# Layer-1 selective scans of a two-layer vision state-space model: decay in PSUM, B in single PSUM banks, the product with C on GpSimd

## The chip, the cores and the metric

The kernel runs on one core of a Trainium2 chip. The metric is the device time of one execution in microseconds (us). Before the change the median of three timed runs is 46,708.61 us (46,704.51 to 46,712.61).

In the profile the engines are PE (TensorE: matrix products), PEld (its loads of weights), DVE (VectorE), ACT (ScalarE), POOL (GpSimd) and SP (SyncE, which issues transfers). Each engine works through its own queue in program order and waits on semaphores for the others.

## The reference, cut to what matters

The input is an image batch, 4 x 128 x 128 pixels with 192 channels. Two residual layers follow each other; each is normalised in groups, projected, convolved, scanned and projected back. The change concerns the scan of layer 1. There every one of 192 channels has 16 states and is scanned in four directions over L = 16,384 tokens (by rows, by rows backwards, by columns, by columns backwards):

```python
def step(state, inp):
    d, b, c, uu = inp
    dA = jnp.exp(d[..., None] * A_neg[:, None, :, :])
    state = dA * state + (d * uu)[..., None] * b[:, :, None, :]
    y = jnp.einsum('kbcn,kbn->kbc', state, c)
    return (state, y)
```

For a channel and a state n: the decay is exp(A * delta), the increment delta * u * B, the output the sum over the 16 states of state times C. B and C depend on token, state, direction and batch, not on the channel. The outputs of the four directions are added. Everything is fp32.

## The kernel before

Layer 0 comes first, then layer 1 in four stages: `in_conv` and `projections` (which write u, delta, B and C of all directions to DRAM), `scans`, and `layer1_out`. Channels lie on the partitions. Layer 1 takes the four batches in two pairs: 2 x 192 channels are three blocks of 128.

`scans` loops over 2 pairs, 3 blocks (i), 4 directions (k), and 16 chunks of T = 1024 tokens: 384 chunks. For each chunk it loads delta (`d`), `u` and 128 rows of B and C (`bt`), and GpSimd forms `du` = d * u (L579). Then it goes through the 16 states n. One state is:

- ScalarE: `dA` = exp(d * A_n) (L593), 128 x 1024, into SBUF (pool `r_3`, three buffers).
- TensorE: row n of B broadcast to the 128 partitions, by a product of `bt` with a column of the identity, stretched over 128 columns (or with `pick` for block 1): `g`, two PSUM banks of 512 columns, from the helper `mm` (L95); pool `r_ps`, two buffers.
- VectorE: `h` = du * g (L605).
- VectorE: the scan `h` = dA * h(previous token) + h, along the tokens (L607), starting from the last value of the chunk before, `st`.
- GpSimd: the last column of `h` copied to `st` for the next chunk (L613).
- VectorE: `hc` = h * C (L617). C comes as `ct`, broadcast by a transfer over the partitions, two states at a time, three buffers (L586).
- TensorE: `hc` times the identity, added up over the 16 states in `Y`, two PSUM banks (L619); pool `r_ps`, two buffers.

After the 16 states VectorE adds `Y` to `ysum` in SBUF (L624, L629 or L636, by direction; the two column directions use a strided pattern at L636).

The text names by B(n), scan(n), hc(n) and Y(n) these products of state n. A product of fp32 with 512 columns is two passes of TensorE, so a state is eight passes: four for B, four for Y.

The order of the instructions on each engine is fixed when the program is built: a scheduler places them by their dependences and by which buffers are free, so the number of buffers of a pool decides how far an engine's queue runs ahead in program order. In this kernel's built order TensorE's queue reads B(n+3), Y(n), B(n+4), Y(n+1) and so on: B is three states ahead. `du` of the next chunk is placed on GpSimd among the copies of the chunk in work, and `ysum` of a chunk on VectorE after the first scan of the next chunk.

[...]

Of the kernel before, what the change touches and what calls it, by code (L numbers as in the profile page):

```python
# [17 lines left out]
L = H * W  # L18
R = 8                # image rows in a chunk
T = R * W            # tokens in a chunk  # L20
NCH = L // T
HC = C // 2          # layer 0 keeps the 192 channels as two halves of 96
NB = 3               # layer 0: 384 inner channels, three blocks of 128
PAD = 5              # reach of the widest dilated convolution
HW_ = W + 2 * PAD
NS = 16              # layer 1: states per channel
DR = 12              # both layers: rank of the step-size projection

# Layer 1 takes the batches in pairs: 2 x 192 channels are three full blocks of 128.
# Block 0: channels 0..127 of the first; block 2: of the second;  # L30
# block 1: channels 128..191 of the first, then of the second.
PAIRS = B // 2
# Weights W[192, 192] for such blocks are six [128, 128] tiles (pair_pack); which tile takes
# which input block to each output block:
AA, MA, MC, AM, CM, MM = range(6)
PAIR_TERMS = (((AA, 0), (MA, 1)), ((AM, 0), (MM, 1), (CM, 2)), ((MC, 1), (AA, 2)))

# Columns of the packed per-channel vectors.
V0_CW, V0_CB, V0_DTB, V0_AL, V0_DS, V0_K, V0_G, V0_B, V0_N = 0, 9, 10, 11, 12, 13, 40, 41, 42
V1_CW, V1_CB, V1_G, V1_B, V1_DTB, V1_DS, V1_AL, V1_N = 0, 9, 10, 11, 12, 16, 20, 84  # L40

# The dilated convolutions as (column of the weights, dy, dx); the three centres are one tap.
TAPS = [
# [9 lines left out]
def segments(first, n, dy):  # L53
    """Rows first..first+n-1 moved by dy and clamped to the image, as runs within one chunk:
    (offset among the n, chunk, row in it, rows, whether it is one row repeated)."""
    runs = []
    for i in range(n):
        src = min(max(first + i + dy, 0), H - 1)
        ch, row = divmod(src, R)
        if runs:  # L60
            o, c, r0, cnt, rep = runs[-1]
            if c == ch and row == r0 and (rep or cnt == 1):
                runs[-1] = (o, c, r0, cnt + 1, True)
                continue
            if c == ch and not rep and row == r0 + cnt:
                runs[-1] = (o, c, r0, cnt + 1, False)
                continue
        runs.append((i, ch, row, 1, False))
    return runs
# [16 lines left out]
class Maker:  # L86
# [3 lines left out]
    def mm(self, out, terms):  # L90
        """out [M, 2, 512] = the sum of lhsT.T @ rhs over terms; rhs has 1024 columns."""
        nc = self.nc
        for h in range(2):
            for i, (lhsT, rhs) in enumerate(terms):
                nc.tensor.matmul(  # L95
                    out[:, h], lhsT, rhs[:, h * 512 : (h + 1) * 512],
                    start=(i == 0), stop=(i == len(terms) - 1),
                )

    def softplus(self, pool, x, bias, one):  # L100
        """log(1 + exp(x + bias)) of a PSUM tile, as max(., 0) + log1p(exp(-|.|));
        log1p(u) is ln(w) + (u - (w - 1)) with w the rounded 1 + u."""
        nc = self.nc
# [14 lines left out]
    def gn_finish(self, pool, psum, stats, p96, eps, out):  # L118
        """bn_stats of every channel [96, 2, n, 6] -> out [96, 2, 2]: mean and
        1/sqrt(var + eps) of the channel's group of six."""  # L120
        nc = self.nc
# [15 lines left out]

# [1 line left out]

# [32 lines left out]

# [1 line left out]

    def layer0(self, xT, x1T, gn_in, gn_out, w, ident, p96, eps, one):
        nc, tc = self.nc, self.tc
        ctx = ExitStack()
        with ctx:
# [23 lines left out]

            # -exp(A_logs), in A_logs' place
            al = vec[:, :, V0_AL : V0_AL + 1]
            nc.scalar.activation(al, al, AF.Exp)
            nc.vector.tensor_scalar_mul(al, al, -1.0)
            # the dilated kernels times their alphas, the centres summed
            for d in range(3):
# [16 lines left out]

            def first_half(b, j):
                """Chunk j up to its scan: xn, xs, xd (projections) and hp (the states, with the
                image's edge columns repeated)."""
                r0 = R * j
# [86 lines left out]
            def second_half(b, j, stats):  # L316
                """Chunk j from its dilated convolutions to the layer's output; reads the states
                of the chunks beside it."""
                r0 = R * j
# [96 lines left out]

# [1 line left out]

    @staticmethod
    def block_parts(p, i):  # L420
        """Block i of pair p: (its partitions, batch, channels)."""
        if i == 1:
            return [(slice(0, 64), 2 * p, slice(128, C)), (slice(64, 128), 2 * p + 1, slice(128, C))]
        return [(slice(0, 128), 2 * p + i // 2, slice(0, 128))]
# [11 lines left out]
    def in_conv(self, x1T, gn, xc, win, vec):  # L436
        """xc[o][p][i]: the convolved input of block i, by rows (o = 0) and by columns (o = 1)."""
        nc, tc = self.nc, self.tc
# [71 lines left out]
    def projections(self, xc, delta, bc, xpw, dtw, dtb2, one):  # L510
        """delta[p][i][k]: the step sizes; bc[p][o]: 128 rows of B and C, those of direction
        2 o + kk and batch e of the pair from row 64 kk + 32 e on."""
        nc, tc = self.nc, self.tc
# [31 lines left out]
    def scans(self, xc, delta, bc, y, ident, alog, dsum):  # L545
        """y[p][i]: the four directions' outputs of block i, summed, by rows."""
        nc, tc = self.nc, self.tc
        with tc.tile_pool(name="r_1", bufs=1) as p1, tc.tile_pool(
            name="r_2", bufs=2
        ) as p2, tc.tile_pool(name="r_3", bufs=3) as p3, tc.tile_pool(  # L550
            name="r_ps", bufs=2, space=PSUM
        ) as ps:
            # Block 1 takes B of the first batch to its first 64 partitions, of the second to the rest.
            pick = p1.tile([128, 2, NS, 128], F32, name="pick")
            for kk in range(2):
                for e in range(2):
# [4 lines left out]
                    )  # L561
            NC_ = 2  # states whose C one load brings
            for p in range(PAIRS):
                for i in range(3):
                    ysum = p1.tile([128, L], F32, tag="ysum", name="ysum")
                    for k in range(4):
# [3 lines left out]
                        for at, j in enumerate(order):  # L570
# [8 lines left out]
                            nc.gpsimd.tensor_tensor(du, d, u, ALU.mult)  # L579
                            Y = ps.tile([128, 2, 512], F32, tag="Y", name="Y")  # L580
                            for n in range(NS):
                                if n % NC_ == 0:
                                    ct = p3.tile([128, NC_, T], F32, tag="ct", name="ct")
                                    for part, b, _ in self.block_parts(p, i):
# [6 lines left out]
                                        )  # L591
                                dA = p3.tile([128, T], F32, tag="dA", name="dA")
                                nc.scalar.activation(  # L593
# [5 lines left out]
                                else:  # L599
                                    r = 64 * kk + 16 * i + n  # L600
                                    lhsT = ident[:, r : r + 1].to_broadcast([128, 128])
                                g = ps.tile([128, 2, 512], F32, tag="g", name="g_B")
                                self.mm(g, [(lhsT, bt)])
                                h = p3.tile([128, T], F32, tag="h", name="h")
                                nc.vector.tensor_tensor(h, du, flat(g), ALU.mult)  # L605
                                way = slice(None) if kk == 0 else slice(None, None, -1)
# [4 lines left out]
                                if at < NCH - 1:  # L611
                                    last = T - 1 if kk == 0 else 0
                                    nc.gpsimd.tensor_copy(  # L613
                                        st[:, n : n + 1], h[:, last : last + 1]
                                    )
                                hc = p3.tile([128, T], F32, tag="hc", name="hc")
                                nc.vector.tensor_tensor(hc, h, ct[:, n % NC_], ALU.mult)  # L617
                                for s in range(2):
# [107 lines left out]
def kernel(ctx: ExitStack, tc: tile.TileContext, w: dict, out: bass.AP):  # L726
# [24 lines left out]

    # layer 1
    xc = [
# [20 lines left out]
    nc.sync.dma_start(vec, w["vec1"].rearrange("(k p) v -> p k v", p=128))  # L774
    # -exp(A_logs), in A_logs' place; twice the step sizes' bias; the directions' D summed
    alog = vec[:, :, V1_AL : V1_AL + 4 * NS]
# [19 lines left out]

# [1 line left out]
def pair_pack(w):  # L798
    """[192, 192] -> [128, 6, 128], the tiles AA, MA, MC, AM, CM, MM."""
    t = np.zeros((128, 6, 128), np.float32)  # L800
    t[:, AA] = w[:128, :128]
    t[:64, MA] = w[128:, :128]
    t[64:, MC] = w[128:, :128]
    t[:, AM, :64] = w[:128, 128:]
    t[:, CM, 64:] = w[:128, 128:]
    t[:64, MM, :64] = w[128:, 128:]
    t[64:, MM, 64:] = w[128:, 128:]
    return t


def block_rows(v):
    """Per-channel rows [192, n] -> [256, n]: those of blocks 0 and 2, then those of block 1."""
    return np.concatenate([v[:128], v[128:], v[128:]])
# [80 lines left out]
```

## Time and profile before

| | |
|---|---|
| median of the timed runs | 46,708.61 us |
| span of the profiled execution, first to last instruction | 46,686.2 us |
| what lies around the span, against that median | 22.4 us |
| layer 0 and the first stages of layer 1, up to the first L605 | 15,702 us |
| scans of layer 1 | 29,159 us |
| `layer1_out` | 1,825 us |
| VectorE, busy in the span | 40,417.4 us (87%) |
| TensorE | 36,537.3 us (78%) |
| ScalarE | 14,711.1 us (32%) |
| GpSimd | 4,422.5 us (9%) |
| mean granted TensorE clock | 0.935 |

No time of the profiled execution beside its span is shown, so its own time is taken as the span and those 22.4 us. The slices of the span show the stages:

```profile
PE   6878778777555788788877887788778877787789
DVE  6777777777944799999999999999999999999952
ACT  3323232332399522222222222222222222222235
POOL 0000000000033200010000000000001000000000
PEclk8888888888778899999999999999999999999999
```

Each digit is the busy share, in tenths, of a fortieth of the span (1,167 us). Layer 0 fills slices 1 to 11; the scans begin in slice 14 and fill the digits 9 of DVE; the last two slices are `layer1_out`. PEclk is the clock that was granted to TensorE, in tenths of full speed.

In a group's row the numbers behind the first bar are the busy time in us and the mean of one instruction in ns; behind the second bar stands the idle time of that engine just before these instructions, and what ended most of it. In a row of the timeline the first two numbers are start and duration in us.

### The profile page before, as it was taken

The numbers are of one execution on the slowest core, as the hardware profiler recorded it, in microseconds if no ns is written. First come the engines' busy times: TensorE is split into PE (matmuls) and PEld (weight loads), VectorE is DVE, ScalarE is ACT, GpSimd is POOL, SyncE is SP. The second block draws the span as 40 slices with busy tenths as digits, with TensorE's granted clock in tenths as the row PEclk, the third lists the DMA queues.
The fourth block names the chain that finished last, engine by engine and source line by source line (L and its number), as shares of the span: only waits on it lengthen the run. The fifth ranks groups of instructions, "written<-read, shape, count | busy, mean of one in ns | idle before, by whom it ended". The sixth has DMA issues, their size and how long they took to land. (4 is left out here: it accounts for less than half of the span.)

```text
span 46686.2 us, 265243 instructions
## 1 busy us (share of the span) xinstructions
PE 36537.3 (78%) x86440; PEld 15672.6 (34%) x86440; DVE 40417.4 (87%) x29807; ACT 14711.1 (32%) x13430; POOL 4422.5 (9%) x8170
## 2 busy tenths in 40 slices
PE   6878778777555788788877887788778877787789
PEld 3334334333222233333333333333333333333345
DVE  6777777777944799999999999999999999999952
ACT  3323232332399522222222222222222222222235
POOL 0000000000033200010000000000001000000000
PEclk8888888888778899999999999999999999999999
DMA  3000000000533333345555333333335555433332
GB/s 99 15 16 16 13 16 16 13 16 26 188 133 121 122 134 132 130 138 134 132 131 136 134 132 130 136 133 132 132 130 139 134 130 131 138 133 132 130 109 80
DMA packets 1411883, 4893.13 MB, mean 105 GB/s; under 512 B 122496, under 2 KB 254464, under 8 KB 1410496
## 3 DMA queue, kind: packets, MB, share of 16 engines
q1 hardware_dynamic: 1398208, 4842.60, 33.9%
q0 software_dynamic: 12288, 33.57, 0.3%
q8 instruction: 683, 11.19, 0.1%
q14 instruction: 704, 5.77, 0.0%
HBM read 4338.82 MB, written 536.88 MB: 104 GB/s over the span
## 5 line engine op out<-in xcount | busy, mean ns | idle before, releaser
L607 DVE TENSOR_TENSOR_SCAN h<-dA,st,h 128x1024 f32<-128x1024 f32 x5760 | 14190.3, 2464 | 0.2
L593 ACT ACTIVATE dA<-d,vec 128x1024 f32<-128x1024 f32 x6144 | 7053.0, 1148 | 22089.0 <-DVE h L607 22088.9
L619 PE MATMUL Y<-hc,ident 128*128 128x512 f32 x24576 | 11762.4, 602 | 76.6 <-DVE hc L617 73.8
L95 PE MATMUL g_B<-bt,ident 128*128 128x512 f32 x16384 | 8432.8, 639 | 3884.7 <-DVE h L605 3867.7
L617 DVE TENSOR_TENSOR hc<-h,ct 128x1024 f32<-128x1024 f32 x6144 | 7517.6, 1224 | 0.5
L605 DVE TENSOR_TENSOR h<-du,g_B 128x1024 f32<-128x1024 f32 x6144 | 7329.4, 1193 | 17.2 <-PE g_B L95 17.2
L619 PEld LDWEIGHTS Y<-hc,ident 128*128 128x128 f32 x24576 | 4800.1, 196 | 6277.1 <-issue 6118.7
L95 PEld LDWEIGHTS g_B<-bt,ident 128*128 128x128 f32 x16384 | 2872.2, 194 | 9244.7 <-DVE h L605 6275.6
L95 PE MATMUL g_B<-bt,pick 128*128 128x512 f32 x8192 | 4187.3, 635 | 1886.3 <-DVE h L605 1881.7
L328 PE MATMUL hf<-hp,diag 128*128 128x512 f32 (+3 forms) x14496 | 4569.1, 473 | 261.3 <-ACT hp L307 209.8
L613 POOL COPY st<-h 128x1 f32<-128x1 f32 x5760 | 1180.0, 205 | 24745.4 <-DVE h L607 24743.8
L328 PEld LDWEIGHTS hf<-hp,diag 128*128 128x128 f32 x14496 | 2452.4, 196 | 2205.8 <-issue 1350.3
L95 PEld LDWEIGHTS g_B<-bt,pick 128*128 128x128 f32 x8192 | 1434.4, 193 | 4542.6 <-DVE h L605 3053.5
L344 DVE SCALAR_TENSOR_TENSOR y<-hp,vec,y 128x1024 f32<-128x1024 f32 (+6 forms) x3264 | 2799.2, 900 | 60.5 <-ACT hp L307 54.3
L114 DVE TENSOR_TENSOR sp_l<-sp_l,sp_rl 128x1024 f32<-128x1024 f32 x576 | 967.2, 1679 | 1178.1 <-ACT sp_l L110 1178.1
L278 DVE SCALAR_TENSOR_TENSOR xs<-xi,vec,xs 128x1024 f32<-128x1024 f32 x1536 | 1898.5, 1276 | 2.3 <-DVE y L344 0.2
L95 PE MATMUL g_dt<-pj,dtw 128*128 128x512 f32 x1536 | 970.1, 774 | 1112.7 <-ACT pj L531 742.8
L113 POOL TENSOR_TENSOR sp_r<-sp_u,sp_r 128x1024 f32<-128x1024 f32 x576 | 1523.4, 2645 | 3146.3 <-DVE sp_r L112 3144.9
L95 PE MATMUL g_xd<-xs,xpw 128*128 128x512 f32 x768 | 609.0, 937 | 1183.9 <-ACT xs L282 967.9
L579 POOL TENSOR_TENSOR du<-d,u 128x1024 f32<-128x1024 f32 x384 | 1259.6, 3280 | 1900.8 <-DVE h L605 1778.5
L348 DVE TENSOR_TENSOR y<-y,hf 128x1024 f32<-128x1024 f32 x192 | 231.9, 1208 | 1168.7 <-PE hf L328 1168.7
L363 ACT ACTIVATE sq<-y 128x1024 f32<-128x1024 f32 x192 | 203.0, 1057 | 3050.3 <-DVE y L361 2968.4
(157 smaller groups left out, 27538.7 us busy)
## 6 DMA issues: line engine op xcount, KB each, us to landing
ct<-bc SPq DMA_DIRECT2D x2048, 1024.0 KB, 5.1
ct<-bc SPq DMA_DIRECT2D x2048, 512.0 KB, 6.4
u<-xc SPq DMA_DIRECT2D x576, 512.0 KB, 3.7
delta<-sp_l SPq DMA_DIRECT2D x384, 512.0 KB, 2.6
d<-delta SPq DMA_DIRECT2D x384, 512.0 KB, 3.5
bt<-bc SPq DMA_DIRECT2D x384, 512.0 KB, 3.9
x<-x1T SPq DMA_DIRECT2D x112, 640.0 KB, 5.9
xa<-xT SPq DMA_DIRECT2D x56, 960.0 KB, 5.8
```

The costliest lines, as they stand in the source:

```text
L95: nc.tensor.matmul(out[:, h], lhsT, rhs[:, h * 512 : (h + 1) * 512], start=(i == 0), stop=(i == len(terms) - 1),)
L113: nc.gpsimd.tensor_tensor(r, u, r, ALU.subtract)
L278: nc.vector.scalar_tensor_tensor(a3, xi[:, t // 3 : t // 3 + R, t % 3 : t % 3 + W], v(k, V0_CW + t), a3, ALU.mult, ALU.add,)
L328: nc.tensor.matmul(hf[:, h, o * W : (o + n) * W], diag[:, k, i], rows_of(hp[ch, k], row, n, rep, PAD + dx, W), start=(i == 0), stop=(i == ...
L344: nc.vector.scalar_tensor_tensor(y3[:, o : o + n], src, v(k, V0_K + col), y3[:, o : o + n], ALU.mult, ALU.add,)
L579: nc.gpsimd.tensor_tensor(du, d, u, ALU.mult)
L593: nc.scalar.activation(dA, d, AF.Exp, scale=alog[:, i % 2, k * NS + n : k * NS + n + 1],)
L605: nc.vector.tensor_tensor(h, du, flat(g), ALU.mult)
L607: nc.vector.tensor_tensor_scan(h[:, way], dA[:, way], h[:, way], 0.0 if at == 0 else st[:, n : n + 1], ALU.mult, ALU.add,)
L613: nc.gpsimd.tensor_copy(st[:, n : n + 1], h[:, last : last + 1])
L617: nc.vector.tensor_tensor(hc, h, ct[:, n % NC_], ALU.mult)
L619: nc.tensor.matmul(Y[:, s], ident, hc[:, s * 512 : (s + 1) * 512], start=(n == 0), stop=(n == NS - 1),)
```

## The change

In `scans`, four things, and no other function that computes:

- `dA` is a tile of the PSUM pool `r_ps` (two banks, two buffers) and no longer of SBUF. ScalarE writes it there, the scan reads it there.
- The broadcast of B is made in single banks: for each half of 512 columns a tile `g` [128, 512], one product (L606), and a VectorE multiplication of that half (L607). `g` has two buffers, so two banks in place of four.
- `Y` moves to a pool of its own, `r_ps1`, with one buffer of two banks. [...]
- `hc` = h * C is made on GpSimd (L619 of the changed file) and no longer on VectorE; the copy of the last column into `st` goes from GpSimd to ScalarE (L615).

The scan is at L609 of the changed file, Y's products at L621, `ysum` at L626, L631 and L638. The rest of the diff takes out comments, which moves lines and no instruction.

```diff
         with tc.tile_pool(name="r_1", bufs=1) as p1, tc.tile_pool(
             name="r_2", bufs=2
         ) as p2, tc.tile_pool(name="r_3", bufs=3) as p3, tc.tile_pool(
-            name="r_ps", bufs=2, space=PSUM
-        ) as ps:
+            name="r_ps1", bufs=1, space=PSUM
+        ) as ps1, tc.tile_pool(name="r_ps", bufs=2, space=PSUM) as ps:
...
-                            Y = ps.tile([128, 2, 512], F32, tag="Y", name="Y")
+                            Y = ps1.tile([128, 2, 512], F32, tag="Y", name="Y")
...
-                                dA = p3.tile([128, T], F32, tag="dA", name="dA")
+                                dA = ps.tile([128, T], F32, tag="dA", name="dA")
...
-                                g = ps.tile([128, 2, 512], F32, tag="g", name="g_B")
-                                self.mm(g, [(lhsT, bt)])
                                 h = p3.tile([128, T], F32, tag="h", name="h")
-                                nc.vector.tensor_tensor(h, du, flat(g), ALU.mult)
+                                for s in range(2):
+                                    half = slice(s * 512, (s + 1) * 512)
+                                    g = ps.tile([128, 512], F32, tag="g", name="g_B")
+                                    nc.tensor.matmul(g, lhsT, bt[:, half], start=True, stop=True)
+                                    nc.vector.tensor_tensor(h[:, half], du[:, half], g, ALU.mult)
...
-                                    nc.gpsimd.tensor_copy(
+                                    nc.scalar.copy(
                                         st[:, n : n + 1], h[:, last : last + 1]
                                     )
                                 hc = p3.tile([128, T], F32, tag="hc", name="hc")
-                                nc.vector.tensor_tensor(hc, h, ct[:, n % NC_], ALU.mult)
+                                nc.gpsimd.tensor_tensor(hc, h, ct[:, n % NC_], ALU.mult)
```

## The prediction

> **What bounds the kernel now.** I read the page's groups and slices first, then a table by stretches of time, then the timeline at single steps, because a share over the whole span says nothing of one stage.
>
> The layer-1 scans run from the first to the last multiplication at L605:
>
> ```profile
> core 0: us, PE busy (x) PEld busy (x) DVE busy (x) ACT busy (x) POOL busy (x), PEclk, DMA share, GB/s
> 15702.33:44861.00 29158.67, 23316.69 (x49144) 9104.35 (x49144) 29113.42 (x18821) 7049.80 (x6141) 2432.56 (x6142) 0.98 0.44 133
> ```
>
> VectorE is busy for 29,113 of 29,159 us: it alone sets this stage. There are 2 pairs x 3 blocks x 4 directions x 16 chunks = 384 chunks, so a chunk costs 29,158.67 / 384 = 75.9 us. The groups that make it:
>
> ```profile
> L607 DVE TENSOR_TENSOR_SCAN h<-dA,st,h 128x1024 f32<-128x1024 f32 x5760 | 14190.3, 2464 | 0.2
> ...
> L617 DVE TENSOR_TENSOR hc<-h,ct 128x1024 f32<-128x1024 f32 x6144 | 7517.6, 1224 | 0.5
> L605 DVE TENSOR_TENSOR h<-du,g_B 128x1024 f32<-128x1024 f32 x6144 | 7329.4, 1193 | 17.2 <-PE g_B L95 17.2
> ...
> L579 POOL TENSOR_TENSOR du<-d,u 128x1024 f32<-128x1024 f32 x384 | 1259.6, 3280 | 1900.8 <-DVE h L605 1778.5
> ```
>
> In the timeline equal instructions recur every 4.51 us (L605 at 30002.04 and 30006.55): that is a state. 16 x 4.51 = 72.2; the rest of the 75.9 is `ysum` (1.2 us, or 2.4 at L636) and one blocked scan per chunk:
>
> ```profile
> 30042.61 1.21 DVE L605 TENSOR_TENSOR h<-du,g_B 128x1024 f32<-128x1024 f32 x1
> ...
> 30043.73 1.23 DVE L617 TENSOR_TENSOR hc<-h,ct 128x1024 f32<-128x1024 f32 x1
> 30043.90 3.26 POOL L579 TENSOR_TENSOR du<-d,u 128x1024 f32<-128x1024 f32 x1 [0.88 <-DVE h L605]
> 30044.86 4.45 DVE L607 TENSOR_TENSOR_SCAN h<-dA,st,h 128x1024 f32<-128x1024 f32 x1
> ```
>
> GpSimd's product waits for VectorE's L617 (3.26 us, its shortest is 2.35), then holds up the scan (4.45 for 2.35). Both have two SBUF inputs. With one input in PSUM there is no such block:
>
> ```profile
> 8043.79 2.36 POOL L113 TENSOR_TENSOR sp_r<-sp_u,sp_r 128x1024 f32<-128x1024 f32 x1 [4.39 <-DVE sp_r L112]
> ...
> 8044.99 1.22 DVE L297 TENSOR_TENSOR sp_l<-sp_l,g_B 128x1024 f32<-128x1024 f32 x1 [1.34 <-ACT dA L294]
> ```
>
> **The change, part by part.** (a) L617 leaves VectorE: 1.13 us of its queue per state. (b) dA in PSUM leaves the scan, like the multiplication, one SBUF input, so the pair above says GpSimd runs at 2.35 us beside it and the 2.1 us block per chunk goes. (c) The multiplication in two halves: L344 takes 1.275 us for 1024 elements and 0.742 for 512, so 512 are 0.53 us. From first half to scan are 1.11 - 0.53 = 0.58 and, the second half being awaited at once, 0.80 (worked out below), instead of 1.11: +0.27 per state. (d) The `st` copy goes to ScalarE, behind the next dA and ahead of the one after it: no cost, since ScalarE is 7,050 us busy of 29,159 and dA(n+2) starts some 5 us before its scan; only a lag beyond that would show. VectorE alone would then need 1.38 + 2.26 = 3.64 us per state, TensorE eight passes of 0.43 = 3.44, GpSimd 2.35. No engine is full at 4.5 us. SP's loads of `ct` keep their order and wait on GpSimd instead of VectorE; with three buffers they are issued some 20 us ahead of need, against 5.1 to 6.4 us to landing.
>
> What decides is (e), TensorE's order. In the built order of the changed kernel nearly every state reads: B(n+1) first half, B(n+1) second half, Y(n), B(n+2) first half, and so on. B was three states ahead of Y; with two single banks it is one ahead, B(n+2) stands behind Y(n), and Y(n) now waits for GpSimd's hc(n); behind B(n+2) wait VectorE's halves. So scan n leads to scan n+2 over five engines' hand-overs:
>
> ```profile
> 40047.42 0.30 PEld L619 LDWEIGHTS Y<-hc,ident 128*128 128x128 f32 x2 [2.37 <-DVE hc L617]
> ...
> 40050.96 0.19 PEld L95 LDWEIGHTS g_B<-bt,ident 128*128 128x128 f32 x1 [0.24 <-issue]
> 40051.22 1.22 DVE L605 TENSOR_TENSOR h<-du,g_B 128x1024 f32<-128x1024 f32 x1 [3.86 <-PE g_B L95]
> ...
> 40052.55 2.29 DVE L607 TENSOR_TENSOR_SCAN h<-dA,h 128x1024 f32<-128x1024 f32 x1
> ```
>
> This shows Y's four passes and B's four from the first load to their end, 40050.96: 3.54 us. The link is: scan start to GpSimd start 2.48 (29999.78 to L613 at 30002.26); product 2.35; GpSimd end to the next engine 0.05 (L113 ends 4025.35, ScalarE starts 4025.39); 3.54; to VectorE 0.20 (passes end 3035.55, L348 starts 3035.75); second half to the dependent scan 1.33 - 0.53 = 0.80. Sum 9.42 us for two states. Even states have one wait more in front of hc (the load of `ct`), 0.07 (a scan's end to L613 is 0.13 with an extra wait, 0.06 without): 9.49. So 4.75 us per state, not 3.6: as long as before. Bounds: 0.15 either way for the hand-overs not seen together.
>
> Chunk: 8 x 9.49 = 75.9. `ysum` stands after the next chunk's first scan and delays the odd states: with S0 the end of the chunk's first scan, the second ends at S0 + 4.78 (slots: `ysum` 1.15, 0.58, 0.80, scan 2.34, less 0.08 of overlap), in two directions of four, with the longer `ysum`, at S0 + 5.97. The next `du` is queued on GpSimd between hc(1) and hc(2); then it ends at 5.97 + 0.13 + 2 x 2.35 = S0 + 10.8, where hc(2) could start at S0 + 9.7: +1.1, on the mean +0.55. The single Y costs nothing: `ysum` is done before Y's first passes. Chunk 76.45, so +0.5 x 384 = +0.2 ms, and the whole stage would stay level. One price is missing in this.
>
> (f) TensorE's clock. Before, its idle gaps are 0.81 us; after the blocked scan they are longer:
>
> ```profile
> 30287.13 1.88 PE L619 MATMUL Y<-hc,ident 128*128 128x512 f32 x4
> 30291.50 3.57 PE L95 MATMUL g_B<-bt,ident 128*128 128x512 f32 x4 [2.49 <-DVE h L605]
> ```
>
> After 2.49 us idle four passes took 3.57 instead of 1.98. Laying the trace's clock changes over the gaps between 16.0 and 44.5 ms: the clock goes to half for 3.41 us in 389 places; never where TensorE was idle for under 1.9 us of the 3.41 before, always above 2.25; I take 2.1. It costs nothing now, since VectorE is behind. In the changed kernel these passes are on the path. Evenly spaced, the gaps would be about 1.2 us and harmless. But they will not be even: the chunk's second scan ends 4.78 us after its first, one half of B(3) stands before Y(1), which shortens the odd link by 0.86, and from state 3 on odd scans end 8.56 + 4.78 - 9.49 = 3.85 us after even ones, then 0.07 less per pair down to 3.64, where VectorE's order stops it. The next even scan is then 5.64 to 5.85 away, and TensorE idles in one piece for that less 3.47 (its passes end 6.07 after the odd scan's end, the next Y begins 2.60 after the even one's): 2.2 to 2.4 us. A free 3.41 us stretch holds 2.1 us of such a gap with chance (3.41 - g + 2(g - 2.1)) / 3.41 = 0.41 to 0.47; each time half of 3.41, less up to 0.15, is lost on the path: 1.6 us. 0.7 x 7 pairs = 5.0 us per chunk (the first pair is spaced more evenly). Bounds: 0 (gaps below 2.1) and 0.6 x 1.7 x 8 = 8. I take 5.0, since the spacing follows from the order.
>
> [...]
>
> Sum: chunk 76.45 + 5.0 = 81.45; (81.45 - 75.93) x 384 = +2.1 ms. The profiled execution spans 46,686.2 us, 22.4 below the median of the timed runs; 46,708.6 + 2,120 = 48,830, rounded to 48,800. Its own range: chance of a slow clock 0.3 to 0.6 per pair, links 0.15 either way: 47.8 to 49.8 ms.
>
> **Rivals.**
> 1. Level: the links as summed, states evenly spaced, clock never halved. 46.9 ms, 46.4 to 47.4 with the 0.15. For it: gaps of 2.2 stand close to 2.1. Against: the spacing above.
> 2. Faster: TensorE's queue does not hold B back, and VectorE's 3.6 us per state decide: 16 x 3.6 + 1.7 = 59.3 per chunk, 40.3 ms. It needs a link under 7.2 us, or B issued before Y. Against: the order is fixed in the program, and 9.42 is measured in pieces. Short of it, any link below 9.3 without slow clock is faster too.
> 3. GpSimd is blocked after all by scans (3.26 us instead of 2.35): links of 10.4, gaps of 3.3, slow clock in three pairs of four: about 93 per chunk, 53 ms. Against: 8043.79.
>
> **How the numbers follow.** Forecast 0.55, level 0.22, faster 0.11, blocked 0.07, between level and forecast 0.05. 0.2% (93 us) is about what these runs tell from no change. Level gives slower 0.13, same 0.05, faster 0.04; so slower 0.55 + 0.13 + 0.07 + 0.05 = 0.80, same 0.05, faster 0.15. The range reaches from the low end of level to the high end of the forecast, 46.4 to 49.8 ms; outside stay rivals 2 and 3.
>
> **What would show it.** Right: hc on GpSimd at 2.35 us; VectorE well below 90% busy in the stage, waiting at the halves for TensorE's B; TensorE's loads for Y waiting for GpSimd's hc; scans no longer at 4.4; the clock of the stage down from 0.98 to about 0.9; two states every 10 us. Wrong: VectorE still full, or the mean hc near 3.3, or clock 0.98 with two states in 9.4.

## The result and the profile after

The changed kernel takes 47,953.92 us in the median of four runs (47,950.95 to 47,957.09), the kernel before 46,706.56 (46,699.25 to 46,712.61): 1.0267 times as long, 95% interval 1.0252 to 1.0282. The forecast was 48,800, within 46,400 to 49,800. The profiled execution spans 47,955.3 us, 1,269 more than before. All but some 20 us of it lies in the layer-1 scans, here from the table of busy times by stretches, with the columns that the same table had above:

```profile
15702.00:46110.00 30408.00, 23694.09 (x49149) 9282.89 (x49150) 23170.87 (x18824) 7408.02 (x11912) 15332.92 (x6528) 0.96 0.42 127
```

VectorE was busy for 29,113 of 29,159 us; now it is for 23,171 of 30,408. It has less to do and the stage is longer: no engine is full any more, so the time is in what they wait for. The groups of the page name it:

```profile
L619 POOL TENSOR_TENSOR hc<-h,ct 128x1024 f32<-128x1024 f32 x6144 | 14450.9, 2352 | 15070.0 <-DVE h L609 11084.1
...
L609 DVE TENSOR_TENSOR_SCAN h<-dA,st,h 128x1024 f32<-128x1024 f32 x5760 | 13534.0, 2350 | 611.1 <-DVE h L607 14.7
L607 DVE TENSOR_TENSOR h<-du,g_B 128x512 f32<-128x512 f32 x12288 | 8253.7, 683 | 6566.4 <-PE g_B L606 6019.1
L621 PEld LDWEIGHTS Y<-hc,ident 128*128 128x128 f32 x24576 | 4474.3, 200 | 14649.6 <-POOL hc L619 11072.6
```

Neither side is blocked: the product with C takes 2,352 ns on GpSimd, the scan 2,350 (its mean was 2,464, with one blocked scan per chunk). VectorE waits 6,566 us ahead of the halves, 6,019 of it for B from TensorE; TensorE's loads for Y wait for GpSimd's hc; hc waits for the scan. That is a ring.

The loss is not spread evenly. The same table for pair 0, block 0, one row per direction (rows, rows backwards, columns, columns backwards; the column after the five engines is the granted TensorE clock):

```profile
15713.24:17022.22 1308.98, 1018.95 (x2045) 404.40 (x2044) 951.59 (x788) 308.27 (x496) 638.37 (x272) 0.93 0.35 122
17022.22:18328.83 1306.61, 1017.99 (x2049) 403.78 (x2048) 948.36 (x784) 308.35 (x496) 636.69 (x272) 0.93 0.35 122
18328.83:19549.13 1220.30, 950.71 (x2048) 367.20 (x2046) 981.32 (x784) 308.35 (x496) 638.87 (x273) 1.00 0.38 131
19549.13:20776.95 1227.82, 957.33 (x2049) 370.52 (x2050) 981.76 (x785) 308.32 (x496) 639.66 (x272) 0.99 0.38 129
```

Sixteen chunks take 1,309 and 1,307 us in the row directions at a clock of 0.93, and 1,220 and 1,228 in the column directions at 1.00 and 0.99. Taken over the whole stage from the starts of the scans, a chunk is 81.71 us in the row directions (75.40 before) and 76.60 in the column directions (76.43 before). 192 x 6.31 + 192 x 0.17 = 1,244 us: the row directions carry nearly all of the loss.

What a row direction looks like, in the timeline (start, duration; in brackets the engine's idle time and what ended it):

```profile
16107.44 2.35 DVE L609 TENSOR_TENSOR_SCAN h<-dA,st,h 128x1024 f32<-128x1024 f32 x1
16108.80 1.99 PE L621 MATMUL Y<-hc,ident 128*128 128x512 f32 x4 [2.38 <-POOL hc L619]
...
16111.75 1.48 DVE L607 TENSOR_TENSOR h<-du,g_B 128x512 f32<-128x512 f32 x2 [1.95 <-PE g_B L606]
...
16113.33 2.35 DVE L609 TENSOR_TENSOR_SCAN h<-dA,st,h 128x1024 f32<-128x1024 f32 x1
...
16116.96 2.35 DVE L609 TENSOR_TENSOR_SCAN h<-dA,st,h 128x1024 f32<-128x1024 f32 x1
16118.31 3.60 PE L621 MATMUL Y<-hc,ident 128*128 128x512 f32 x4 [2.25 <-POOL hc L619]
...
16122.96 1.48 DVE L607 TENSOR_TENSOR h<-du,g_B 128x512 f32<-128x512 f32 x2 [3.65 <-PE g_B L606]
16123.54 1.88 PE L621 MATMUL Y<-hc,ident 128*128 128x512 f32 x4
16124.53 2.35 DVE L609 TENSOR_TENSOR_SCAN h<-dA,st,h 128x1024 f32<-128x1024 f32 x1
```

The scans come in bunches of two: 16113.33 and 16116.96 are 3.63 us apart, then a longer pause. In that pause TensorE idles in one piece, 2.38 and 2.25 us. The first gap is followed by passes at full speed (1.99 us), the second by passes at half speed (3.60), and VectorE waits 3.65 us for B instead of 1.95. Two states take 16116.96 - 16107.44 = 9.52 us in the first case, and from 16113.33 to 16124.53 it is 11.20.

In a column direction the same instructions are spaced evenly, TensorE's gaps are about 1 us, and the clock stays up:

```profile
30005.30 1.99 PE L621 MATMUL Y<-hc,ident 128*128 128x512 f32 x4 [0.84 <-POOL hc L619]
...
30010.22 1.98 PE L621 MATMUL Y<-hc,ident 128*128 128x512 f32 x4 [1.22 <-POOL hc L619]
```

Laid over the starts of the scans, the trace's clock changes give the price. A slow window is a stretch of 3.41 us in which the trace has the clock at half; a pair meets one if it begins between the pair's first scan and the next pair's. Of 1,152 pairs of states in row chunks (states 2 to 14), 658 meet no slow window and take 9.52 us in the median; 494 meet one and take 11.20. Of 1,152 pairs in column chunks 26 meet one. A whole row chunk has 3.3 windows, a column chunk 0.2; the 178 column chunks without any take 76.3 us.

### The profile page after: what moved, and what is told of

It reads as the page before. It is cut to its first block, busy times and chain, and to the rows that moved or that the text cites. A ratio compares the mean times of both kernels' runs of the same rounds, so it can differ in the third digit from the quotient of the medians.

```text
span 47955.3 us, 272544 instructions
## 1 busy us (share of the span) xinstructions
PE 36887.1 (77%) x86440; PEld 15856.4 (33%) x86440; DVE 34469.5 (72%) x29807; ACT 15057.7 (31%) x19190; POOL 17314.8 (36%) x8554
## 4 chain that ended last, share of the span: by engine, by line
PE 27%; DVE 16%; POOL 14%; issue 9%; ACT 6%; DMA 1%; POOLq 0%; SPq 0%; DVEq 0%; ACTq 0%
PE Y L621 15%; POOL hc L619 14%; DVE h L609 11%; PE g_B L606 10%; DVE h L607 4%; ACT L108 1%; ACT L110 1%; ACT sp_u L108 1%; ACT sp_u L105 1%; ACT sp_l L110 1%; PE g_dt L95 0%; DMA x<-x1T 0%; PE g_o L702 0%; ACT dA L593 0%; PE g_o L705 0%
## 5 line engine op out<-in xcount | busy, mean ns | idle before, releaser
L619 POOL TENSOR_TENSOR hc<-h,ct 128x1024 f32<-128x1024 f32 x6144 | 14450.9, 2352 | 15070.0 <-DVE h L609 11084.1
L621 PE MATMUL Y<-hc,ident 128*128 128x512 f32 x24576 | 13138.0, 661 | 6635.6 <-POOL hc L619 6620.2
L609 DVE TENSOR_TENSOR_SCAN h<-dA,st,h 128x1024 f32<-128x1024 f32 x5760 | 13534.0, 2350 | 611.1 <-DVE h L607 14.7
L607 DVE TENSOR_TENSOR h<-du,g_B 128x512 f32<-128x512 f32 x12288 | 8253.7, 683 | 6566.4 <-PE g_B L606 6019.1
L621 PEld LDWEIGHTS Y<-hc,ident 128*128 128x128 f32 x24576 | 4474.3, 200 | 14649.6 <-POOL hc L619 11072.6
L606 PE MATMUL g_B<-bt,ident 128*128 128x512 f32 x16384 | 7845.5, 599 | 61.6 <-DVE h L607 51.8
L615 ACT COPY st<-h 128x1 f32<-128x1 f32 x5760 | 1103.2, 192 | 21543.2 <-DVE h L609 21543.2
L593 ACT ACTIVATE dA<-d,vec 128x1024 f32<-128x1024 f32 x6144 | 6837.4, 1113 | 1444.9 <-DVE h L609 1444.7
L606 PEld LDWEIGHTS g_B<-bt,ident 128*128 128x128 f32 x16384 | 3206.5, 197 | 4329.7 <-issue 3730.8
L606 PE MATMUL g_B<-bt,pick 128*128 128x512 f32 x8192 | 3930.7, 600 | 24.0 <-DVE h L607 24.0
L606 PEld LDWEIGHTS g_B<-bt,pick 128*128 128x128 f32 x8192 | 1602.5, 197 | 2155.0 <-issue 1838.5
```

Of the source, the lines that this page charges most:

```text
L593: nc.scalar.activation(dA, d, AF.Exp, scale=alog[:, i % 2, k * NS + n : k * NS + n + 1],)
L606: nc.tensor.matmul(g, lhsT, bt[:, half], start=True, stop=True)
L607: nc.vector.tensor_tensor(h[:, half], du[:, half], g, ALU.mult)
L609: nc.vector.tensor_tensor_scan(h[:, way], dA[:, way], h[:, way], 0.0 if at == 0 else st[:, n : n + 1], ALU.mult, ALU.add,)
L615: nc.scalar.copy(st[:, n : n + 1], h[:, last : last + 1])
L619: nc.gpsimd.tensor_tensor(hc, h, ct[:, n % NC_], ALU.mult)
```

## The experiments

The theory: the order of TensorE's queue ties each state to the one two before it (9.5 us for two), whatever the engines could do; where the odd scans bunch behind the even ones, TensorE's clock halves on top of that (in 494 of the 1,152 pairs above). The rivals: the row directions are slow for another reason; GpSimd's product or TensorE's load holds the states at 4.7 us; the banks do; the place of dA has no effect. Times in us, the ratio against the kernel before on the same chip (46,693 to 46,707); a chunk is the mean distance from one chunk's first scan to the next one's in the trace.

| run | us | ratio to before | chunk |
|---|---|---|---|
| changed kernel | 47,953.9 | 1.0267 [1.0252, 1.0282] | 79.2 |
| 1 longer row sum | 47,288.5 | 1.0125 [1.0109, 1.0140] | 77.4 |
| 9 the same, three buffers for u | 47,006.3 | 1.0064 [1.0049, 1.0079] | 76.6 |
| 2 shorter column sum | 48,644.4 | 1.0414 [1.0397, 1.0431] | 81.0 |
| 3 Y two states later | 42,342.6 | 0.9066 [0.9052, 0.9079] | 64.6 |
| 5 four banks for B | 47,597.8 | 1.0194 [1.0177, 1.0211] | 78.2 |
| 6 Y over the chunk's end | 40,935.2 | 0.8766 [0.8753, 0.8780] | 60.9 |
| 4 hc back on VectorE | 47,651.4 | 1.0203 [1.0187, 1.0218] | 78.4 |
| 7 hc alone on GpSimd | 50,405.1 | one run | 85.6 |
| 8 dA back in SBUF | 48,645.5 | one run | 81.0 |
| 10 run 6 with dA in SBUF | 47,336.7 | 1.0134 [1.0117, 1.0151] | 77.5 |

### More work for VectorE in the row directions (runs 1 and 9)

```diff
+                            if k < 2:
+                                spare = p1.tile([128, T], F32, tag="spare", name="spare")
+                                nc.vector.tensor_tensor(spare, du, flat(Y), ALU.add)
                             if k == 0:
                                 nc.vector.scalar_tensor_tensor(
```

> One operation more on VectorE behind each chunk of the two row directions: a sum of du and Y into a spare tile, some 1.2 us, right beside ysum, so that the row directions have as long a piece there as the column directions (2.4 us). In the changed kernel a chunk takes 81.7 us in the row directions and 76.6 in the column directions, and 2.95 slow clock windows fall into a row chunk, 0.19 into a column chunk. Theory (the short ysum lets the odd scans bunch behind the even ones, TensorE idles over 2 us in one piece and its clock halves): row chunks fall to 76.6 us and the windows vanish, 192 x 5.1 us = 980 us less, 46,970 us, though VectorE has more to do. Rival (row directions are slower for another reason): 192 x 1.2 us more, 48,180 us. No difference if ysum's length does not matter.

(The windows in this expectation are counted in the first 75 us of each chunk; over the whole chunk they are 3.3 and 0.2.)

With 192 operations of 1.2 us more on VectorE the kernel is 665 us faster than the changed one, where 980 were expected. Directions 0 and 1 of block 0:

```profile
15715.34:17016.40 1301.06, 1007.16 (x2045) 395.31 (x2044) 971.90 (x804) 308.24 (x496) 636.42 (x271) 0.94 0.35 123
17016.40:18236.92 1220.52, 950.46 (x2047) 365.99 (x2045) 981.07 (x801) 308.30 (x496) 640.06 (x272) 1.00 0.38 131
```

Direction 1 became what a column direction is (1,220 us, clock 1.00). Direction 0 did so in block 1 alone (76.7 us a chunk) and stayed at 81.7 in blocks 0 and 2. There the timeline shows GpSimd's `du` of the next chunk standing between two products:

```profile
15881.24 2.35 POOL L619 TENSOR_TENSOR hc<-h,ct 128x1024 f32<-128x1024 f32 x1 [3.54 <-DVE h L609]
...
15882.35 2.35 DVE L609 TENSOR_TENSOR_SCAN h<-dA,st,h 128x1024 f32<-128x1024 f32 x1
...
15883.55 2.36 POOL L579 TENSOR_TENSOR du<-d,u 128x1024 f32<-128x1024 f32 x1
...
15885.86 2.35 POOL L619 TENSOR_TENSOR hc<-h,ct 128x1024 f32<-128x1024 f32 x1
```

The scan that the last of these products reads had ended at 15884.7; the product began at 15885.86. This state's link grows by 0.9 us, scan 4 comes 5.48 us after scan 3 instead of 4.55, and the bunching is back. `du` stands there because the `ysum` of direction 0 reads u and so frees its buffer late. In block 1 it stands at the same place in 20 chunks of direction 0, and hc(2) is as late; but there the first half of B(4) is ahead of Y(2) in TensorE's queue, which takes up the delay: scan 4 comes 4.62 us after scan 3, and these chunks take 76.3 us. So the place of `du` does harm only together with this order of the passes. Run 9 gives u a third buffer, which moves `du` ahead of hc(1) in these chunks:

```diff
-                            u = p2.tile([128, T], F32, tag="u", name="u")
+                            u = p3.tile([128, T], F32, tag="u", name="u")
```

> The run with the longer row sums, and u with three buffers instead of two. In that run the chunks of direction 1, and of direction 0 in block 1, fell to 76.7 us, those of direction 0 in blocks 0 and 2 stayed at 81.7. There GpSimd's queue has the next chunk's du between hc(1) and hc(2), because u's buffer is freed late (ysum of direction 0 reads u); hc(2) then starts 0.9 us late, and the odd scans bunch after all. With a third u buffer the built order has du between hc(0) and hc(1) in these chunks as well. Theory: the 64 chunks of direction 0 in blocks 0 and 2 fall from 81.7 to 76.7 us, 320 us less than the 47,290 of that run: 46,970 us, and all chunks between 76.2 and 77. Rival (direction 0 of these blocks is slow for another reason): 47,290 us again.

Measured 47,006, with 76.8 us a row chunk, 76.5 a column chunk, and 81 slow windows in the stage instead of 670. The means by block and direction lie between 76.2 and 77.1 us, as expected, but for direction 0 of block 2 (77.9). Direction 0 of block 0 now:

```profile
15718.88:16946.71 1227.83, 956.93 (x2034) 369.69 (x2032) 976.72 (x799) 307.10 (x495) 633.55 (x270) 0.99 0.38 129
```

So the loss of the row directions is the spacing of the scans, and with it the clock. Extra work that spreads the scans, with `du` moved out of the way, takes out nearly all of it.

### Less work for VectorE in the column directions (run 2)

```diff
-                                yv = ysum.rearrange("p (h w) -> p w h", w=W)[
-                                    :, R * j : R * (j + 1)
-                                ]
                                 nc.vector.tensor_tensor(
-                                    yv, yv, Y.rearrange("p s (w h) -> p (s w) h", h=H), ALU.add
+                                    ysum[:, cols], ysum[:, cols], flat(Y), ALU.add
                                 )
```

> The column directions' ysum reads and writes ysum in its stored order instead of the transposed one, so 1.2 us instead of 2.4 (the column directions are summed at wrong places). Theory: the column directions then bunch like the row directions, 192 x 5.1 us = 980 us more, 48,930 us, though VectorE has less to do; some 3 slow clock windows in every chunk. Rival (row directions are slower for another reason): 192 x 1.2 us less, 47,720 us.

Measured 48,644: 690 us more, where 980 were expected and the rival said less. Direction 2 of block 0, 1,220 us at clock 1.00 in the changed kernel:

```profile
18316.91:19627.00 1310.09, 1019.75 (x2050) 404.45 (x2049) 946.90 (x784) 308.25 (x496) 637.40 (x273) 0.93 0.35 122
```

In blocks 0 and 2 the column chunks are at 81.5 to 82.0 us, as expected. The shortfall lies in block 1, where column chunks came out at 79.5 to 80.6 us with 2.1 to 2.3 windows, and the row chunks, which this edit leaves alone, fell from 81.4 to 79.5 as well. In block 1 the built order has `du` at another place: in 86 of its 128 chunks between hc(2) and hc(3), where it delays an odd scan (scan 5 mostly comes 4.6 us after scan 4 there, not 3.6). These chunks take 78.7 us in the mean; the 38 with `du` between hc(0) and hc(1) take 81.7. Why the build places it there stays open.

### Y two states later in TensorE's queue (run 3)

```diff
+                                late.append((n, hc))
+                                while len(late) > (0 if n == NS - 1 else 2):
+                                    m, hm = late.pop(0)
-                                for s in range(2):
-                                    nc.tensor.matmul(
-                                        Y[:, s], ident, hc[:, s * 512 : (s + 1) * 512],
-                                        start=(n == 0), stop=(n == NS - 1),
-                                    )
+                                    for s in range(2):
+                                        nc.tensor.matmul(
+                                            Y[:, s], ident, hm[:, s * 512 : (s + 1) * 512],
+                                            start=(m == 0), stop=(m == NS - 1),
+                                        )
```

> The passes for Y are issued two states later within the chunk, so that Y(n) stands behind B(n+2) instead of B(n+1) in TensorE's queue; buffers and all other work as in the changed kernel. Theory (the queue's order sets the time): the same link of 9.4 us now leads to the third scan on, 3.1 us a state, less than VectorE's 3.64, which then decides. At the chunk's end Y is flushed, so B of the next chunk waits for hc(15): 2.48 + 2.35 + 0.05 + 1.72 + 0.86 + 0.20 + 1.38 = 9.0 us from the last scan to the first. Chunk 15 x 3.64 + 9.0 = 63.6, up to 66 with a slow clock there; 384 x (79.2 - 64) = 5,800 us less: 42,100 us, 41,500 to 43,000. Rival (the hand-overs, GpSimd's product or TensorE's load of 3.44 us a state hold it at 4.7 us a state whatever the order): 47,500 to 48,500 us.

Measured 42,343 (expected 42,100): 5,600 us less, from nothing but the order in which TensorE's passes are issued. The timeline:

```profile
20001.30 2.35 DVE L610 TENSOR_TENSOR_SCAN h<-dA,st,h 128x1024 f32<-128x1024 f32 x1
...
20003.57 1.26 DVE L608 TENSOR_TENSOR h<-du,g_B 128x512 f32<-128x512 f32 x2
20003.82 2.36 POOL L620 TENSOR_TENSOR hc<-h,ct 128x1024 f32<-128x1024 f32 x1 [1.22 <-DVE h L610]
...
20004.93 2.35 DVE L610 TENSOR_TENSOR_SCAN h<-dA,st,h 128x1024 f32<-128x1024 f32 x1
```

Scans 3.63 us apart, the halves follow the scan with no wait, and B's passes for a later state run while GpSimd forms hc. Within the chunk the median from scan to scan is 3.63 everywhere; from the last scan to the next chunk's first it is 10.1 on the mean (expected 9.0), since Y is flushed there. The expected sum left out `ysum`, which stands ahead of the next halves in VectorE's queue: the median is 9.5 us in the row directions and 10.7 with the longer `ysum` of the column directions. The stage has 14 slow windows.

### Four banks for B, one buffer for dA (run 5)

```diff
-                                dA = ps.tile([128, T], F32, tag="dA", name="dA")
+                                dA = ps1.tile([128, T], F32, tag="dA", name="dA")
...
-                                    g = ps.tile([128, 512], F32, tag="g", name="g_B")
+                                    g = ps.tile([128, 512], F32, tag="g", name="g_B", bufs=4)
```

> dA keeps one PSUM buffer (two banks) and g gets four single banks instead of two; B is then three states ahead of Y in TensorE's queue, as in the kernel before. Theory (the lead of B decides): the link over GpSimd no longer sets the time. dA(n+1) must wait for the end of scan n: 2.35 + 0.05 + 1.11 + 0.05 = 3.6 us a state, 3.8 with the copy of the state in front of it on ScalarE; chunk 16 x 3.8 + 1.8 = 62.6 us, 384 x (79.2 - 62.6) = 6,400 us less, 41,600 us, 40,800 to 42,500. Rival (GpSimd's product, not the order, is what holds the states back): 47,500 us or more.

A miss by 6,000 us: 47,598. The expectation was wrong in its first sentence. B leads by three states only in the stage's first few; in 3,609 of the first 4,000 states of the trace the order of the passes is the old one, with B one state ahead of Y. With twice the banks the timeline looks as before:

```profile
30036.65 1.98 PE L621 MATMUL Y<-hc,ident 128*128 128x512 f32 x4 [0.96 <-POOL hc L619]
30038.47 1.88 PE L606 MATMUL g_B<-bt,ident 128*128 128x512 f32 x4
...
30039.60 1.48 DVE L607 TENSOR_TENSOR h<-du,g_B 128x512 f32<-128x512 f32 x2 [0.73 <-PE g_B L606]
```

Y waits for GpSimd, B stands behind Y, the halves wait for B; pairs without a slow window take 9.52 us again. The 356 us under the changed kernel go with fewer slow windows (486 instead of 670; at 1.6 us each that is 300); they are missing mainly in direction 0 of blocks 0 and 2 (76 us a chunk), where the first half of B(4) stands ahead of Y(2). Run 3 had the order and not the banks, this run the banks and not the order: it is the order.

### Y issued over the chunk's end (run 6)

Run 3 with the pending products of Y kept in one list over all chunks of a block; `ysum` and the next tile Y are issued where their products come out of that list.

> As the run with Y two states later, but the delayed passes of Y and ysum go over the chunk's end: the last two of a chunk are issued in the next one, ysum behind them. Theory: VectorE full, 16 x 3.64 + 1.8 = 60.0 us a chunk, 384 x (79.2 - 60.0) = 7,400 us less than the changed kernel: 40,600 us, 40,100 to 41,500. TensorE then has 55 of 60 us of a chunk to do. Rival (TensorE or the loads of ct become the bound near 4 us a state): 42,500 us.

Measured 40,935: faster than both kernels, 0.8766 [0.8753, 0.8780] times the one before. Of a chunk's 60.9 us the states take 3.63 each; the remaining waits stand behind the first two states, where Y's first products wait for `ysum` (the single Y buffer) and the clock halves in 262 places, 239 of them behind the second scan of a chunk.

### The product back on VectorE (run 4)

```diff
-                                nc.gpsimd.tensor_tensor(hc, h, ct[:, n % NC_], ALU.mult)
+                                nc.vector.tensor_tensor(hc, h, ct[:, n % NC_], ALU.mult)
```

> Only the product with C goes back to VectorE; dA in PSUM, the single banks and the copy of the states on ScalarE stay. Theory: VectorE needs 3.64 + 1.13 = 4.77 us a state and the link over Y and B is 2.34 + 1.2 + 0.06 + 3.54 + 0.20 + 0.80 = 8.1 us for two states, so VectorE decides: 16 x 4.77 + 1.7 = 78.0 us a chunk, up to 1 more where du and hc meet, 47,500 to 47,900 us; the clock near 0.98. Rival (the product on GpSimd is what costs): level with the kernel before less the blocked scan, 46,000 us.

Measured 47,651, inside the theory's range. VectorE is full again, at 4.72 us a state, and the clock is up:

```profile
15707.00:45815.00 30108.00, 23195.96 (x49146) 9026.29 (x49144) 29771.91 (x24963) 7395.70 (x11902) 950.22 (x382) 0.98 0.43 129
```

That is still 945 us over the kernel before. 4.72 us a state against 4.51 before are 3.4 us a chunk, in the place where the halves are; the vanished block of one scan per chunk (2.1 us) gives back less, and in its place one hc per chunk is held up (the mean of hc on VectorE is 1,285 ns, its median 1,225: 1.0 us a chunk). That makes 2.3 of the 2.5 us by which a chunk is longer than before. Moving the product to GpSimd takes VectorE off the bound, and the ring that takes its place costs 0.8 us a chunk more.

### Where dA lies (runs 7, 8 and 10)

Run 7 is the kernel before with `nc.gpsimd` instead of `nc.vector` at L617. Runs 8 and 10 put dA back into SBUF, run 8 in the changed kernel, run 10 in run 6:

```diff
-                                dA = ps.tile([128, T], F32, tag="dA", name="dA")
+                                dA = p3.tile([128, T], F32, tag="dA", name="dA")
```

> The kernel before with one change: the product with C on GpSimd; dA stays in SBUF, g in pairs of banks. Theory (a scan with two SBUF inputs and GpSimd block each other, as at du in the kernel before): hc takes some 3.3 us instead of 2.35, scans 4.4 instead of 2.35, a state 1.11 + 4.45 = 5.6 us, a chunk 90 us: 52,000 us. Rival (no block worth naming): VectorE needs 3.4 us a state, 39,000 us.

> The changed kernel with dA back in an SBUF tile of three buffers; all else as changed. Theory: the scan has two SBUF inputs again and blocks, or is blocked by, GpSimd's hc: hc 3.3 us, scans up to 4.45; the link over five engines grows from 9.5 to 11 or 12 us for two states, chunk 90 to 95 us: 52,500 to 54,500 us. Rival (the place of dA is without effect): 47,950 us.

Both came out cheaper than expected: 50,405 (52,000) and 48,646 (52,500 to 54,500; the rival's 47,950 was nearer). The groups of run 8:

```profile
L619 POOL TENSOR_TENSOR hc<-h,ct 128x1024 f32<-128x1024 f32 x6144 | 14592.8, 2375 | 14952.8 <-DVE h L609 12125.7
L609 DVE TENSOR_TENSOR_SCAN h<-dA,st,h 128x1024 f32<-128x1024 f32 x5760 | 14835.9, 2576 | 623.8 <-DVE h L607 27.9
```

Products of 2,375 ns and scans of 2,576: hardly blocked. I had priced every scan like the one that meets `du`. At some 4.75 us a state a product of 2.35 fits between two scans of 2.35, and the ring already spaces them so. In run 7 hc has a mean of 2,381 ns and the scan 2,732, and most states take 4.7 us; VectorE waits 6,321 us for B. What else makes its chunks 85.6 us long stays open. Run 10 takes the ring away:

> The fastest run so far (Y issued two states later, over the chunk's end: 60.9 us a chunk) with dA back in an SBUF tile of three buffers. In the run with dA in SBUF at the changed kernel's order the price was small (hc 2.38 us instead of 2.35, scans 2.58): at 4.75 us a state a product of 2.35 fits between two scans of 2.35. Theory (a scan and a product with only SBUF inputs do not run at the same time): a state needs 2.35 + 2.35 = 4.70 us here, du 2.35 more per chunk: 77.6 to 80 us a chunk, 40,935 + 384 x 17.9 = 47,800 us, 47,000 to 48,800; scans or hc then show the blocked time as their own length, 3.6 to 4.7 us. Rival (the block is only a fraction of a microsecond, as in that run): 42,000 us.

Measured 47,337, in the theory's range, 6,400 us over run 6:

```profile
L651 POOL TENSOR_TENSOR hc<-h,ct 128x1024 f32<-128x1024 f32 x6144 | 15947.0, 2600 | 12206.7 <-DVE h L641 9641.0
L641 DVE TENSOR_TENSOR_SCAN h<-dA,st,h 128x1024 f32<-128x1024 f32 x5760 | 18787.9, 3262 | 623.7 <-ACT dA L625 30.2
```

```profile
30002.62 2.35 POOL L651 TENSOR_TENSOR hc<-h,ct 128x1024 f32<-128x1024 f32 x1 [2.32 <-DVE h L641]
30003.73 3.40 DVE L641 TENSOR_TENSOR_SCAN h<-dA,st,h 128x1024 f32<-128x1024 f32 x1
...
30007.36 2.36 POOL L651 TENSOR_TENSOR hc<-h,ct 128x1024 f32<-128x1024 f32 x1 [2.38 <-DVE h L641]
30008.41 3.45 DVE L641 TENSOR_TENSOR_SCAN h<-dA,st,h 128x1024 f32<-128x1024 f32 x1
```

The scan is issued at 30003.73, but lasts until 2.2 us after hc's end at 30004.97: so nearly all of its 2.35 us of work must lie behind the product. The states take 4.67 and 4.73 us in turn, the sum of the two works. So dA in PSUM is worth 0.7 ms at the changed kernel's order (one run) and 6.4 ms once the order is right.

## The prediction, step by step

- **(a), (b) VectorE's queue and the block.** Right. hc 2,352 ns, scan 2,350, `du` 2,353 on the mean (3,280 before). Rival 3 fell: the product and the scan with dA in PSUM ran side by side. The median scan took 2,350 ns with dA in PSUM, against 2,339 with dA in SBUF before. Run 10 shows that the block is real where both read SBUF alone (scan 3,262 ns, hc 2,600 on the mean).
- **(c) The halves.** Right: 3.64 forecast, and wherever nothing else holds VectorE the scans are 3.63 us apart (bunched pairs, runs 3 and 6).
- **(d) The state's copy and the loads of `ct`.** Right that they cost nothing: in runs 3 and 6 the same copies and loads keep up with 3.63 us a state.
- **(e) TensorE's order.** Right, and the main cause: 9.42 and 9.49 us forecast for two states, 9.52 measured; column chunks without a slow window take 76.3 us, against 76.45 forecast. That is nearer than the working deserves: 0.55 of the 76.45 were for a delay by `du` that did not arise (next point). Run 3 turns the order alone and gains 5.6 ms. Rival 2 (VectorE decides, 40.3 ms) named this condition, "B issued before Y"; run 6 fulfils it and takes 40.9 ms.
- **The next `du` between hc(1) and hc(2).** Wrong for the directions that it was priced in. In the column directions, with the longer `ysum`, the built order has `du` ahead of hc(0) in blocks 0 and 2 and later in the chunk, behind hc(2) or after, in block 1, so the 1.1 us do not arise. It stands between hc(1) and hc(2) in direction 0 of blocks 0 and 2 alone, where u is freed late. Run 1 shows that this place can matter, not by its own 0.9 us, but by bringing the bunching back.
- **(f) The clock.** Right where it was worked out, wrong in its reach. In the row directions 43% of the pairs met a slow window (forecast 0.41 to 0.47), at 1.68 us each (1.6), gaps of 2.2 to 2.4 us: 81.71 us a chunk against 81.45. But the bunching was derived from "the chunk's second scan ends 4.78 us after its first", and the prediction itself gives 5.97 for "two directions of four, with the longer `ysum`". Put into the same formula, 8.56 + 5.97 - 9.49 = 5.04 us: evenly spaced, gaps near 1 us, no slow clock. The trace has 4.97 there. So the step "0.7 x 7 pairs = 5.0 us per chunk" should have been taken for 192 chunks and not for 384. That is nearly the whole error: rows (81.71 - 81.45) x 192 = +50, columns (76.60 - 81.45) x 192 = -931; the sum was 48,830, less 880 is 47,950. The kernel's time so lies between rival 1 and the forecast, an outcome that the prediction gave a chance of 0.05. That it still falls into the forecast's own 47.8 to 49.8 ms is luck: the lower bound there stood for a smaller chance of a slow clock in every direction, not for half the directions without one.
- **The rivals by halves.** Rival 1 ("Level") is what the column directions did, the forecast what the row directions did. Runs 1 and 9 turn the row directions into Level by added work, run 2 turns the column directions into the forecast by less.
- **What would show it.** VectorE at 76% and waiting for B, TensorE's loads waiting for hc, scans no longer at 4.4: as said. The stage's clock is 0.96 and not 0.9, for the reason above (0.93 in the row directions).

## What to carry to other kernels

When work is moved to an idle engine, follow what the new producer's consumer has queued behind it: an in-order queue that holds "use of the late result" ahead of "input of a later step" makes a ring, and issuing the use two steps later was worth 12% here, while twice the banks without that order were worth 0.7%. Read the order in the middle of the loop, not at its start. And when several equal links interleave, work out their spacing for every variant of the loop, because a microsecond at the loop's edge can decide whether an engine idles in one piece or in two (here 1.2 us of `ysum`: 81.71 against 76.60 us a chunk).

## What the hardware showed that I had not expected

- **In these scans the clock halved on a grid, and TensorE's idle time sorted the slow windows sharply.** In the changed kernel the 670 slow windows all begin on one raster of 3.413 us. Idle time of TensorE within the raster's preceding stretch (from the starts of the passes, 0.43 us each; stretches at full speed alone) sorts them: from 1.0 to 2.0 us none of some 3,200 was followed by a slow one, from 2.0 to 2.2 us about a quarter of some 385, from 2.3 us on all of some 425. The counts shift somewhat with the exact place of the stretch's ends; none below 2.0 us and all from 2.3 us on do not.
- **More work was faster.** 192 spare operations on VectorE took 665 us off, and taking 1.2 us off each of 192 sums added 690 us.
- **Two engines with SBUF inputs alone took turns, and the profile booked the wait as length.** In run 10 the scan's mean is 3,262 ns and hc's 2,600, for work of 2,350 each; a state takes 4.7 us. With dA in PSUM, in the changed kernel, both took 2,350.
